# Index loads on other queues, routing and attention products in four groups of partitions, and a new order at the start of a four-layer graph network kernel

## The chip, the cores and the metric

The kernel runs on one core of a Trainium2 chip. The metric is the device time of one execution in microseconds (us), the median over runs; lower is better. A core has a matrix engine (TensorE, PE in the profile, with its weight loads listed as PEld), a vector engine (VectorE, DVE), a scalar engine (ScalarE, ACT), a general engine (GpSimd, POOL), a sequencer for transfers (SyncE, SP) and 16 DMA engines that these queues share. The whole program is one launch of about 40,000 instructions.

## The reference

512 nodes with 768 features pass four layers, and every layer adds a graph network, a token mixer and a feed-forward part to `x`. All four graph networks use the same list of 8704 edges (`src`, `dst`, two edge types, and 256 features for each edge). Cut to what the change touches:

```python
edge_index = jnp.stack([src, dst])
xn = _layernorm(x, axis=-1)
# layer 0, graph network: edges are projected, and summed at their destination
edge_proj = edge_features @ We.T + be
msgs = nodes[src] + nodes[dst] + edge_proj
agg = jax.ops.segment_sum(msgs, dst, num_segments=n)
...
# layers 0 and 2, feed-forward: each token goes to one of 8 experts
logits = xt @ Ws + bs
routes = jnp.argmax(jax.nn.softmax(logits, axis=-1), axis=-1)
...
# layers 1 and 3, graph network: attention over edges from two projections per node and head
qi = oi @ q ; kj = oj @ k
alpha = jax.nn.leaky_relu(qi + kj, NEG_SLOPE)
...
# layer 3, feed-forward: 16 experts, each takes its 64 best tokens
scores = jax.nn.sigmoid(x @ gate_weight.T)
topk_score, topk_ids = jax.lax.top_k(scores.T, capacity)
```

## The kernel before

The program is traced in Python and its instructions are ordered by a list scheduler. The scheduler keeps an order for each engine. It takes what it thinks is ready first, and among ready instructions what the program writes first. At run time every engine executes its own list in that order, and semaphores hold an instruction back until its inputs are there. A tile whose memory belonged to a closed pool waits for the last user of that memory. `tc.issue_after(i)` puts what its block traces on the engine of `i` behind `i` in that engine's list, without a wait.

**Start (`Net.__init__`, L179 to L221).** POOL issues the load of `x` (1536 KB) and of `cols` (all small columns of weights and biases, 210 KB), and then makes constants. Four constants are made on DVE: `sel`, `identb`, `lower` and part of `number`.

**Counting (`counts`, L371 to L516).** The four index arrays come in by POOL's queue (L391) and are cast to float (`ind`, L392). `worth` (L399 to L401) encodes the edge types. The edges lie in 68 columns of 128. For each column `j` DVE makes a one-hot `ohd` of its destinations (L465) and three weighted one-hots `so` of its sources (L468, three buffers). PE multiplies them into six accumulators (L471). This is done in four quarters, for `h` (half of the sources) and `g` (half of the columns): 34 columns with six bf16 products of 512 columns each. The accumulators are opened by a product with `onesb` (L462). At the end of a quarter ACT and DVE take the accumulators apart into digits (L236, L238, L478 to L449). Then follows a quarter of the 34 calls of `features(q)` (L411 to L425): a load of two columns of edge features `ea` (two buffers, by SP), a split of them into three bf16 parts on ACT and DVE alternately (L416, L417, L418, L419), and twelve products with `ohd` (L424). In the program `net.norm` of the first layer (L359 to L363) comes after `counts`, but its inputs are ready early.

**Narrow products.** In six places `xn` transposed (`xnT`, six chunks of 128 x 512, float32) is multiplied by a weight with only 6 to 24 columns, by `self.acc` (L320): the routers of `moe` in layers 0 and 2 (8 columns, `wg`, from `cols`), the attention projections of `rgat` in layer 1 twice (24 and 6 columns, `V`), of `gnn3` in layer 3 (24 columns), and the router of `ffn3` (16 columns, `gw`, from `cols`). The result has one row for each weight column and 512 columns. It is copied out (`loT`, `qkT`) and turned to one row per node by four transposes `self.tr` (L325).

**Order around them.** In `moe` and `ffn3` everything that follows needs the router's result, so PE has nothing else to do. In `rgat` and `gnn3` a generator (`side`, or `beside`) runs between other products on PE. In `ffn3` the weights of the experts (384 loads of 1152 KB) stream by SP into ten buffers `w`; SP issues a load as soon as a buffer is free. `ffn3` calls `rank` for the first two experts, then `choose`, `gather` and the first `up` (L1794), which frees the first buffers. The tile `first` (L1655) is a small sigmoid whose only purpose is to have the table of that function in ACT.

Of the kernel before, what the change touches and what calls it, by code (L numbers as in the profile page):

```python
# [10 lines left out]
F32 = mybir.dt.float32  # L11
# [63 lines left out]

def _layout(i):
# [32 lines left out]
    for f, n, g in (("f0", "L0_ffn", "Ws"), ("f2", "L2_ffn", "Wg")):  # L109
        col(f + "_wg", _thin(i[f"{n}_{g}"]))  # L110
        a[f + "_w1"] = np.stack([_blocks(w)[0, 0] for w in i[n + "_W1"]])
        a[f + "_w2"] = _rows(i[n + "_W2"])
        a[f + "_b2"] = np.ascontiguousarray(i[n + "_b2"])
        col(f + "_b1", _col(i[n + "_b1"]))
# [31 lines left out]
    col("f3_gw", _thin(i["L3_ffn_gate_weight"].T))  # L146
# [18 lines left out]
class Net:  # L165
    def __init__(self, ctx, tc, dram, at, out):
        self.tc, self.nc, self.d, self.at, self.out = tc, tc.nc, dram, at, out
        nc = self.nc
        self.cw = ExitStack()
        self.wp = self.cw.enter_context(tc.tile_pool(name="wp", bufs=6, side="right"))  # L170
        self.keep = ctx.enter_context(tc.tile_pool(name="keep", bufs=1))
        self.small = ctx.enter_context(tc.tile_pool(name="small", bufs=4))
        self.rowp = self.cw.enter_context(tc.tile_pool(name="rowp", bufs=2, side="right"))
        self.pp = ctx.enter_context(tc.tile_pool(name="pp", bufs=8, space=PSUM))
        self.dp = ctx.enter_context(tc.tile_pool(name="dp", bufs=1, space=DRAM))
        self.turn = 0
        keep = self.keep
        self.x = keep.tile([P, NT, D], F32, name="x")
        nc.gpsimd.dma_start(self.x, dram["x"].rearrange("(t p) d -> p t d", p=P))  # L179
        self.cols = keep.tile([P, dram["cols"].shape[1]], F32, name="cols")  # L180
        nc.gpsimd.dma_start(self.cols, dram["cols"])
        self.ident = keep.tile([P, P], F32, name="ident")
        make_identity(nc, self.ident)


        self.sel = keep.tile([96, 32], BF16, name="sel")
        for i in range(3):
            nc.vector.tensor_copy(self.sel[32 * i : 32 * i + 32, :], self.ident[:32, :32])
        self.bias3 = self.rowp.tile([96, 2, D], BF16, name="bias3", bufs=1)
        nc.gpsimd.memset(self.bias3, 0.0)  # L190
        self.which = 0
        self.ones = keep.tile([P, P], F32, name="ones")
        nc.gpsimd.memset(self.ones, 1.0)
        self.eps = keep.tile([P, 1], F32, name="eps")
        nc.gpsimd.memset(self.eps, LN_EPS)
        self.shift = keep.tile([P, 1], F32, name="shift")
        nc.gpsimd.memset(self.shift, -0.472)

        self.io16 = keep.tile([P, 16], F32, name="io16")
        nc.gpsimd.iota(self.io16, pattern=[[1, 16]], base=0, channel_multiplier=0, allow_small_or_imprecise_dtypes=True)  # L200
        self.io8 = self.io16[:, :8]
        self.me = keep.tile([P, 1], F32, name="me")
        nc.gpsimd.iota(self.me, pattern=[[0, 1]], base=0, channel_multiplier=1, allow_small_or_imprecise_dtypes=True)
        self.identb = keep.tile([P, P], BF16, name="identb")
        nc.vector.tensor_copy(self.identb, self.ident)
        self.big0 = keep.tile([P, 1], F32, name="big0")
        nc.gpsimd.memset(self.big0, -BIG)
        self.onesb = keep.tile([P, P], BF16, name="onesb")
        nc.gpsimd.memset(self.onesb, 1.0)
        self.wq1 = keep.tile([P, KC, 32], F32, name="wq1")  # L210
        self.gate = None
        self.lower = keep.tile([P, P], BF16, name="lower")
        with tc.tile_pool(name="init", bufs=1) as ip:
            io = ip.tile([P, P], F32, name="io")
            nc.gpsimd.iota(io, pattern=[[1, P]], base=0, channel_multiplier=0, allow_small_or_imprecise_dtypes=True)
            nc.vector.tensor_scalar(self.lower, io, self.me, None, OP.is_gt)

        self.number = keep.tile([P, NT, 2], BF16, name="number")
        nc.vector.tensor_copy(self.number[:, :, 0], self.me.to_broadcast([P, NT]))
        for t in range(NT):  # L220
            nc.gpsimd.memset(self.number[:, t, 1:2], float(t * P))  # L221

# [98 lines left out]

    def tr(self, out, in_):

        k = in_.shape[0]
        self.nc.tensor.transpose(out, in_, self.ident[:k, :k])  # L325
# [26 lines left out]
    def norm1(self, x, out, t):  # L352
# [8 lines left out]
        nc.scalar.activation(r, mv[:, 1:2], AF.Sqrt, bias=self.eps)  # L361
# [9 lines left out]
    def counts(self, c0, g0):  # L371
# [10 lines left out]
        with ExitStack() as c:  # L382
# [7 lines left out]
            for n, a in enumerate(("src", "dst", "edge_type_3", "edge_type_4")):  # L390
                nc.gpsimd.dma_start(raw[:, n, :], d[a].rearrange("(p j) -> p j", p=P))  # L391
# [10 lines left out]
            io = one.tile([P, N], I16, name="io")  # L402
            nc.gpsimd.iota(io, pattern=[[1, N]], base=0, channel_multiplier=0)
# [6 lines left out]
            def features(q):  # L410
# [7 lines left out]
                nc.scalar.copy(part[:, 1], ea)  # L418
# [38 lines left out]
            for h in range(2):  # L457
                digit = {}
                for g in range(2):
# [3 lines left out]
                    for j in range(g * HJ, (g + 1) * HJ):  # L463
# [3 lines left out]
                        for n in range(3):  # L467
                            nc.vector.tensor_scalar(so[:, n, :], io[:, h * 256 : (h + 1) * 256], ind[:, 0, j : j + 1],  # L468
                                                    worth[:, n, j : j + 1], OP.is_equal, OP.mult)
# [3 lines left out]
                    for (t, n), p in acc.items():  # L473
# [12 lines left out]
                        if g == 1:  # L486
                            finish(h, t, n, lo, hi, *digit[t, n])

                    for q in range((2 * h + g) * EJ // 8, (2 * h + g + 1) * EJ // 8):
                        features(q)  # L490
# [199 lines left out]
    def moe(self, f, act, xn, bs=None):  # L690
# [5 lines left out]
        with ExitStack() as c:  # L696
            one = c.enter_context(tc.tile_pool(name=f + "_one", bufs=1))
            two = c.enter_context(tc.tile_pool(name=f + "_two", bufs=2))
            xnT = one.tile([P, KC, N], F32, name="xnT")
# [8 lines left out]
            wg = self.col(f + "_wg", 0, KC * E).rearrange("p (k e) -> p k e", k=KC)  # L708
            p = self.ps()
            self.acc(p[:E], [(wg[:, k, :], xs[k]) for k in range(KC)])  # L710
            loT = one.tile([E, N], F32, name="loT")
            if bs is None:
                nc.vector.tensor_copy(loT, p[:E])
            else:
                nc.vector.tensor_scalar(loT, p[:E], self.col(bs, 0, 1, E), None, OP.add)
            p = self.ps()
            for t in range(NT):
                self.tr(p[:, t * E : (t + 1) * E], loT[:, t * P : (t + 1) * P])
            lo = one.tile([P, NT, E], F32, name="lo")
            nc.vector.tensor_copy(lo, p[:, : NT * E].rearrange("p (t e) -> p t e", t=NT))  # L720
# [423 lines left out]
    def fold(self, wq, l, H):  # L1144
# [19 lines left out]
        def turn(V, vt):  # L1164
            for a in range(2):
# [3 lines left out]
                nc.scalar.copy(V[:, 3 * a : 3 * a + 3],  # L1169
# [4 lines left out]
    def rgat(self, xT, l, H, V, C, done, between=None):  # L1174
# [4 lines left out]
        with ExitStack() as c:  # L1179
# [6 lines left out]
            qkT = one.tile([J, N], F32, name="qkT")  # L1186
# [8 lines left out]
            p = self.ps()  # L1195
            self.acc(p[:J], [(V[:, k].rearrange("p r h -> p (r h)"), xT[:, k, :]) for k in range(KC)])
            nc.scalar.copy(qkT, p[:J])
# [4 lines left out]
            def side():  # L1202
                p = self.ps()
                for t in range(NT):
                    self.tr(p[:, t * J : (t + 1) * J], qkT[:, t * P : (t + 1) * P])
                nc.scalar.copy(qk.rearrange("p t r h -> p (t r h)"), p[:, : NT * J])
                self.parts(qk3, qkT, qkT, mid, self.copies, nc.vector.tensor_sub)
# [60 lines left out]
    def gnn1(self, V1, xnT):  # L1268
        nc, tc, d = self.nc, self.tc, self.d
        with ExitStack() as c:  # L1270
# [34 lines left out]
            V2 = one.tile([P, KC, 3, 2], F32, name="V2")  # L1305
# [230 lines left out]
    def fold3(self, one):  # L1536
# [7 lines left out]
        V = one.tile([P, KC, 2 * H], F32, name="V")  # L1544
# [10 lines left out]
    def gnn3(self, c, xnT, V):  # L1555
# [19 lines left out]
        qkT = one.tile([2 * H, N], F32, name="qkT")  # L1575
# [5 lines left out]
        p = self.ps()  # L1581
        self.acc(p[: 2 * H], [(V[:, k, :], xnT[:, k, :]) for k in range(KC)])
        nc.scalar.copy(qkT, p[: 2 * H])
        for t in range(NT):
# [7 lines left out]
            if t == 0:  # L1592
                q = self.ps()
                for u in range(NT):
                    self.tr(q[:, u * 2 * H : (u + 1) * 2 * H], qkT[:, u * P : (u + 1) * P])
                nc.scalar.copy(qk.rearrange("p t r h -> p (t r h)"), q[:, : NT * 2 * H])
                self.parts(qk3, qkT, qkT, mid, self.copies, nc.vector.tensor_sub)
# [42 lines left out]
    def ffn3(self, xn, xnT, there):  # L1640
# [5 lines left out]
        with ExitStack() as c:  # L1646
# [8 lines left out]
            nc.scalar.activation(first, self.eps, AF.Sigmoid)  # L1655
# [10 lines left out]
            gw = self.col("f3_gw", 0, KC * NX).rearrange("p (k e) -> p k e", k=KC)  # L1666
            p = self.ps()
            self.acc(p[:NX], [(gw[:, k, :], xnT[:, k, :]) for k in range(KC)])
            loT = one.tile([NX, N], F32, name="loT")
            nc.vector.tensor_copy(loT, p[:NX])  # L1670
            p = self.ps()
            for t in range(NT):
                self.tr(p[:, t * NX : (t + 1) * NX], loT[:, t * P : (t + 1) * P])
            sc = one.tile([P, NT, NX], F32, name="sc")
            nc.scalar.activation(sc, p[:, : NT * NX].rearrange("p (t e) -> p t e", t=NT), AF.Sigmoid)
# [191 lines left out]
def tile_net(ctx, tc, dram, at, out, only=ALL):  # L1867
# [10 lines left out]
    with ExitStack() as ck, ExitStack() as c0:  # L1878
# [4 lines left out]
        with tc.tile_pool(name="L0", bufs=1) as pool:  # L1883
            xnT = pool.tile([P, KC, N], F32, name="xnT")
            with tc.tile_pool(name="L0n", bufs=1) as p2:
                xn = p2.tile([P, NT, D], F32, name="xn")
                net.norm(net.x, xn)
# [8 lines left out]
    with tc.tile_pool(name="L1", bufs=1) as pool, ExitStack() as keep:  # L1896
# [6 lines left out]
        V1 = pool.tile([P, KC, 3, 8], F32, name="V1")  # L1903
# [46 lines left out]
```

## Time and profile before

| | |
|---|---|
| median of 3 runs | 4281.39 us (4278.18 to 4281.85) |
| the profiled execution, its own time | 4283.03 us |
| its span, first to last instruction | 4281.2 us |
| mean granted TensorE clock | 0.988 |
| PE busy | 4117.0 us (96%) |
| DVE busy | 1299.7 us (30%) |
| ACT, POOL busy | 659.5 us (15%), 268.9 us (6%) |
| moved by DMA | 710.30 MB, 166 GB/s in the mean |

The span is what the trace covers; 1.8 us of the execution's own time lie around it. Busy time on PE counts pipelined matrix products until their modelled end, so 96% does not mean that PE runs at its peak. A share over the whole span says little here, because the stages have different limits: the first 25 us hardly use PE, and the last 1100 us move weights at 420 GB/s. So the prediction reads the stages one by one.

### The profile page before, as it was taken

What the parts mean: (1) busy time and instruction counts of PE and PEld (TensorE: products, weight loads), DVE (VectorE), ACT (ScalarE), POOL (GpSimd) and SP (SyncE); (2) the same over time, 40 slices, a digit from 0 to 9 for tenths busy, and PEclk for the clock granted to TensorE, in tenths of its full rate; (3) what the DMA queues carried; (4) which work ended last, traced back from release to release, by engine and by line L of the source; (5) the groups of instructions that cost most, each with busy time, mean ns of one, the idle gap of its engine ahead of it and who ended that gap; (6) DMA issues with size and microseconds to landing.
All of it is one profiled execution on the core that took longest, in us unless ns stands there. A gap on an engine that the chain in (4) does not pass through costs nothing. (4 is left out here: it accounts for less than half of the span.)

```text
span 4281.2 us, 40171 instructions
## 1 busy us (share of the span) xinstructions
PE 4117.0 (96%) x16392; PEld 2100.7 (49%) x16392; DVE 1299.7 (30%) x3120; ACT 659.5 (15%) x1241; POOL 268.9 (6%) x316
## 2 busy tenths in 40 slices
PE   7989999999989999999999999989999999999998
PEld 3434555554445566755644444445654444444443
DVE  7772111112432125513220101035841122122211
ACT  2121200001312223411200000022610000000000
POOL 1120000001022010000000000021100000000000
PEclk9999999999999999999999999989999999999999
DMA  3111011111047112211201111063079999999998
GB/s 111 52 61 57 23 45 66 67 56 53 18 169 293 38 60 72 107 45 55 106 34 67 45 55 56 0 261 136 1 288 420 419 420 420 420 417 420 419 421 363
DMA packets 98955, 710.30 MB, mean 166 GB/s; under 512 B 12032, under 2 KB 12096, under 8 KB 29392
## 3 DMA queue, kind: packets, MB, share of 16 engines
q1 hardware_dynamic: 77776, 601.13, 35.3%
q0 software_dynamic: 16512, 93.97, 5.8%
q10 hardware_dynamic: 4480, 12.58, 0.8%
q8 instruction: 132, 2.16, 0.2%
q14 instruction: 55, 0.45, 0.0%
HBM read 685.09 MB, written 22.54 MB: 165 GB/s over the span
## 5 line engine op out<-in xcount | busy, mean ns | idle before, releaser
L1794 PE MATMUL ps<-w,xg 128*64 128x384 f32 x3072 | 566.0, 489 | 5.0 <-DMA w<-in_f_Wg_dram 3.0
L1794 PEld LDWEIGHTS ps<-w,xg 128*64 128x64 f32 x3072 | 234.1, 137 | 297.2 <-issue 271.0
L1427 PE MATMUL ps<-aT,w 128*128 128x512 f32 x864 | 372.3, 592 | 0.0
L1810 PE MATMUL ps<-w,hT 128*64 128x384 f32 x1536 | 321.0, 490 | 6.3 <-ACT hT L238 2.5
L320 PE MATMUL ps<-xnT,w 128*128 128x512 f32 (+1 forms) x732 | 320.3, 594 | 0.3 <-ACT xnT L238 0.2
L1427 PEld LDWEIGHTS ps<-aT,w 128*128 128x128 f32 x864 | 164.2, 190 | 203.6 <-issue 202.3
L320 PE MATMUL ps<-w,xnT 128*128 128x384 f32 x672 | 221.6, 486 | 0.2 <-DVE xnT L236 0.2
L320 PEld LDWEIGHTS ps<-xnT,w 128*128 128x128 f32 (+1 forms) x732 | 133.7, 184 | 174.7 <-issue 171.3
L1810 PEld LDWEIGHTS ps<-w,hT 128*64 128x64 f32 x1536 | 132.1, 136 | 169.1 <-issue 143.9
L368 DVE TENSOR_TENSOR x<-x,ps 128x384 f32<-128x384 f32 x224 | 123.4, 553 | 295.0 <-PE ps L320 223.6
L320 PE MATMUL ps<-C,parts 128*128 128x512 bf16 x864 | 189.8, 381 | 4.0 <-DVE inv L1449 4.0
L320 PE MATMUL ps<-w,hT 128*128 128x384 f32 x552 | 184.7, 490 | 3.9 <-ACTq L895 3.9
L471 PE MATMUL ps<-ohd,so 128*128 128x512 bf16 x816 | 181.9, 383 | 2.8 <-DVE so L468 2.8
L320 PEld LDWEIGHTS ps<-w,xnT 128*128 128x128 f32 x672 | 127.0, 190 | 88.6 <-issue 4.7
L1437 DVE TENSOR_TENSOR aT<-inv,ps 128x512 f32<-128x512 f32 x72 | 49.5, 688 | 367.2 <-PE ps L320 367.2
L1797 ACT ACTIVATE h<-ps 128x384 f32<-128x384 f32 x64 | 31.4, 491 | 794.8 <-PE ps L1794 794.8
L1798 DVE TENSOR_TENSOR h<-h,ps 128x384 f32<-128x384 f32 x64 | 35.5, 554 | 377.6 <-PE ps L1794 377.6
L320 PEld LDWEIGHTS ps<-w,hT 128*128 128x128 f32 x552 | 103.1, 190 | 81.4 <-ACT xbT L238 7.6
L320 PE MATMUL ps<-w,aT 128*128 128x384 f32 (+1 forms) x416 | 139.6, 486 | 0.5 <-DVE aT L236 0.4
L320 PEld LDWEIGHTS <-parts 128*128 128x128 bf16 x864 | 84.9, 98 | 110.0 <-issue 11.0
L320 PE MATMUL ps<-xnT,sw 128*128 128x512 f32 x288 | 138.3, 611 | 0.0
L468 DVE TENSOR_SCALAR so<-io,ind,worth 128x256 bf16<-128x256 int16 x408 | 121.7, 355 | 35.5 <-PE ps L471 35.4
(499 smaller groups left out, 4804.4 us busy)
## 6 DMA issues: line engine op xcount, KB each, us to landing
w<-in_f_Wg_dram SPq DMA_DIRECT2D x128, 1152.0 KB, 14.5
w<-in_f_Wu_dram SPq DMA_DIRECT2D x128, 1152.0 KB, 15.2
w<-in_f_Wd_dram SPq DMA_DIRECT2D x128, 1152.0 KB, 16.0
w<-in_g_w_dram SPq DMA_DIRECT2D x54, 1152.0 KB, 5.1
w<-in_m_wqkv_dram SPq DMA_DIRECT2D x24, 1152.0 KB, 6.6
w<-in_g_t_dram SPq DMA_DIRECT2D x12, 1152.0 KB, 5.8
w<-in_m_wp_dram SPq DMA_DIRECT2D x8, 1152.0 KB, 5.3
ea<-in_edge_attr_dram SPq DMA_DIRECT2D x34, 256.0 KB, 2.7
```

Source lines behind the costliest of these rows:

```text
L320: self.nc.tensor.matmul(out, a, b, start=n == 0, stop=n == len(pairs) - 1)
L368: self.nc.vector.tensor_add(xs, xs, p)
L468: nc.vector.tensor_scalar(so[:, n, :], io[:, h * 256 : (h + 1) * 256], ind[:, 0, j : j + 1], worth[:, n, j : j + 1], OP.is_equal, OP.mult)
L471: nc.tensor.matmul(p, so[:, n, t * P : (t + 1) * P], ohd[:, j, :], start=False, stop=j == (g + 1) * HJ - 1)
L1427: nc.tensor.matmul(outs[nb * 3 + f], w[:, k, f * P : (f + 1) * P], xT[:, k, :], start=first and k == 0, stop=last and k == KC - 1)
L1437: nc.vector.tensor_mul(aT[:, f, :], inv[:, r, :], p)
L1794: nc.tensor.matmul(p[a * 64 : a * 64 + 64, :HW], xg[:, k, a * CAP : (a + 1) * CAP], ws[b][a][:, k, :], start=k == 0, stop=k == KC - 1)
L1797: nc.scalar.activation(h, pg[:, :HW], AF.Silu)
L1798: nc.vector.tensor_mul(h, h, pu[:, :HW])
L1810: nc.tensor.matmul(po[nb][a * 64 : a * 64 + 64, :HW], hT[:, f * P + a * 64 : f * P + a * 64 + 64], wd[a][:, f, nb * HW : (nb + 1) * HW], s ...
```

## The change

- **Indices.** The four index loads leave POOL's queue; `src` and `edge_type_3` go by SP, `dst` and `edge_type_4` by ACT. The int16 iota `io` and `onesb` are made first on POOL, ahead of the issue of `x` and `cols`.
- **Order of DVE at the start.** The four constants made on DVE move to a function `constants`, which is called with `net.norm` behind `begun`: the last `so` of the third quarter on DVE, and the last `part` of the second quarter on ACT. The DVE work of the first quarter's `features` stands behind the last `so` of the third column (`j` = 2).
- **Narrow products.** Weights are padded to 32 columns. The six chunks go to four groups of 32 output partitions (`narrow`): chunks 0 to 3 open a group each, chunks 4 and 5 add to groups 0 and 1. The four groups are added and turned to rows per node by four products with `fours`, four stacked 32 x 32 identities (`narrow_tm`). In `rgat` and `gnn3` one more product with `fours` makes the sum in rows per weight column.
- **Router weights.** `wg` and `gw` leave `cols` and get loads of their own (96 KB each): `wg` by ACT at the start of `moe`, `gw` by POOL in `ffn3`.
- **Sigmoid.** `first` stands behind `self.root`, the last square root of the norm before it on ACT.

```diff
+        self.onesb = keep.tile([P, P], BF16, name="onesb")
+        nc.gpsimd.memset(self.onesb, 1.0)
+        self.io = keep.tile([P, N], I16, name="io")
+        nc.gpsimd.iota(self.io, pattern=[[1, N]], base=0, channel_multiplier=0)
         nc.gpsimd.dma_start(self.x, dram["x"].rearrange("(t p) d -> p t d", p=P))
...
+        self.fours = keep.tile([P, 32], F32, name="fours")
+        for i in range(4):
+            nc.gpsimd.tensor_copy(self.fours[32 * i : 32 * i + 32, :], self.ident[32 * i : 32 * i + 32, 32 * i : 32 * i + 32])
...
+    def constants(self):
+        nc = self.nc
+        for i in range(3):
+            nc.vector.tensor_copy(self.sel[32 * i : 32 * i + 32, :], self.ident[:32, :32])
+        nc.vector.tensor_copy(self.identb, self.ident)
+        nc.vector.tensor_scalar(self.lower, self.io[:, :P], self.me, None, OP.is_gt)
+        nc.vector.tensor_copy(self.number[:, :, 0], self.me.to_broadcast([P, NT]))
...
+    def narrow(self, w, xs):
+        p = self.ps()
+        for k in range(KC):
+            g = 32 * (k % 4)
+            self.nc.tensor.matmul(p[g : g + 32], w[:, k, :], xs[k], start=k < 4, stop=k + 4 >= KC)
+        return p
+
+    def narrow_tm(self, four, n):
+        p = self.ps()
+        for t in range(NT):
+            self.acc(p[:, t * n : (t + 1) * n], [(four[:, t * P : (t + 1) * P], self.fours[:, :n])])
+        return p[:, : NT * n].rearrange("p (t n) -> p t n", t=NT)
...
-        nc.scalar.activation(r, mv[:, 1:2], AF.Sqrt, bias=self.eps)
+        self.root = nc.scalar.activation(r, mv[:, 1:2], AF.Sqrt, bias=self.eps).ins
...
             for n, a in enumerate(("src", "dst", "edge_type_3", "edge_type_4")):
-                nc.gpsimd.dma_start(raw[:, n, :], d[a].rearrange("(p j) -> p j", p=P))
+                (nc.sync, nc.scalar)[n % 2].dma_start(raw[:, n, :], d[a].rearrange("(p j) -> p j", p=P))
...
                         for n in range(3):
-                            nc.vector.tensor_scalar(so[:, n, :], ...
+                            if j == 3 and n == 0 and h == 0:
+                                made["third"] = made["so"].ins
+                            made["so"] = nc.vector.tensor_scalar(so[:, n, :], ...
...
+                    if h == 1 and g == 0:
+                        self.begun = made["so"].ins, made["part"].ins
                     for q in range((2 * h + g) * EJ // 8, (2 * h + g + 1) * EJ // 8):
-                        features(q)
+                        if h == g == 0:
+                            with tc.issue_after(made["third"]):
+                                features(q)
+                        else:
+                            features(q)
...
             # moe
+            wg = one.tile([P, KC, 32], F32, name="wg")
+            nc.scalar.dma_start(wg.rearrange("p k e -> p (k e)"), d[f + "_wg"])
...
-            self.acc(p[:E], [(wg[:, k, :], xs[k]) for k in range(KC)])
-            loT = one.tile([E, N], F32, name="loT")
+            p = self.narrow(wg, xs)
+            loT = one.tile([P, N], F32, name="loT")
...
-            for t in range(NT):
-                self.tr(p[:, t * E : (t + 1) * E], loT[:, t * P : (t + 1) * P])
-            nc.vector.tensor_copy(lo, p[:, : NT * E].rearrange("p (t e) -> p t e", t=NT))
+            nc.vector.tensor_copy(lo, self.narrow_tm(loT, E))
...
             # rgat, in side(); gnn3 alike
-                for t in range(NT):
-                    self.tr(p[:, t * J : (t + 1) * J], qkT[:, t * P : (t + 1) * P])
-                nc.scalar.copy(qk.rearrange("p t r h -> p (t r h)"), p[:, : NT * J])
-                self.parts(qk3, qkT, qkT, mid, self.copies, nc.vector.tensor_sub)
+                self.acc(p[:J], [(self.fours[:, :J], qkT)])
+                nc.scalar.copy(qk.rearrange("p t r h -> p t (r h)"), self.narrow_tm(qkT, J))
+                self.parts(qk3, p[:J], qkT[:J], mid, self.copies, nc.vector.tensor_sub)
...
             # ffn3
-            nc.scalar.activation(first, self.eps, AF.Sigmoid)
+            with self.tc.issue_after(self.root):
+                nc.scalar.activation(first, self.eps, AF.Sigmoid)
+            gw = one.tile([P, KC, 32], F32, name="gw")
+            nc.gpsimd.dma_start(gw.rearrange("p k e -> p (k e)"), d["f3_gw"])
...
+            p = self.narrow(gw, self.chunks(xnT))
+            loT = one.tile([P, N], F32, name="loT")
+            nc.vector.tensor_copy(loT, p)
             sc = one.tile([P, NT, NX], F32, name="sc")
-            nc.scalar.activation(sc, p[:, : NT * NX].rearrange("p (t e) -> p t e", t=NT), AF.Sigmoid)
+            nc.scalar.activation(sc, self.narrow_tm(loT, NX), AF.Sigmoid)
...
-                net.norm(net.x, xn)
+                with tc.issue_after(net.begun[0]), tc.issue_after(net.begun[1]):
+                    net.constants()
+                    net.norm(net.x, xn)
```

## The prediction

> **What bounds the kernel now.** I read the page's 40 slices first. PE is at 9 almost everywhere, so a gain has to come from PE time or from stretches where PE stands still. Then I asked for PE's waits and the timeline of the start, then for the timeline around each of the six narrow products, and last for the tables by stage. PE's waits between 25 and 345 us (columns: total, times, longest) begin with this:
>
> ```profile
> PE ps L424 <- DVE ohd L465: 17.1, 1, 17.1
> PE ps L424 <- DVE part L419: 5.9, 6, 2.9
> PE ps L424 <- ACT part L418: 4.5, 3, 3.5
> PE ps L471 <- DVE so L468: 2.8, 4, 1.3
> ```
>
> One wait of 17.1 us ends at the first one-hot. The timeline (start, us, engine, line) tells why it is late:
>
> ```profile
> 0.73 0.86 SPq L414 DMA_DIRECT2D ea<-in_edge_attr_dram  x2
> ...
> 3.62 1.24 ACT L416 CAST part<-ea 128x512 bf16<-128x512 f32 x2 [1.62 <-DMA ea<-in_edge_attr_dram]
> ...
> 7.09 1.06 POOL L391 DMA_DIRECT2D so<-in_edge_type_dram  x2
> ...
> 16.43 1.48 DVE L359 BATCH_NORM_STATS2 st<-x 128x6 f32<-128x384 f32 x3 [9.39 <-DMA x<-in_x_dram]
> ...
> 24.34 0.27 DVE L392 CAST ind<-so 128x272 f32<-128x272 int32 x1
> ...
> 27.70 12.65 PE L471 MATMUL ps<-ohd,so 128*128 128x512 bf16 x55
> ```
>
> DVE stands until 16.43 for `x`, since the norm is ahead of the indices in its list, and works off the norm and four constants until 24.3. The indices were issued last on POOL's queue, behind `x`. Then comes the cast. From 25.6 PE is the bound of the columns; only the ends of the second and fourth quarter are DVE's (stretch, then busy us of PE, PEld, DVE, ACT, POOL, clock, DMA share):
>
> ```profile
> 25.00:60.00 35.00, 34.39 (x152) 15.23 (x152) 34.20 (x136) 0.00 (x0) 0.00 (x0) 1.00 0.07 30
> ...
> 300.00:310.00 10.00, 8.01 (x24) 2.74 (x24) 10.00 (x18) 4.10 (x8) 3.37 (x4) 0.73 0.33 106
> ```
>
> The router of layer 0, and two other places where PE runs in column groups or on small outputs:
>
> ```profile
> 1226.62 5.32 PE L320 MATMUL ps<-xnT,cols 128*8 128x512 f32 x12 [0.24 <-DVE xnT L236]
> ...
> 1232.77 0.41 PE L325 MATMUL ps<-ident,loT 8*128 8x8 f32 x4 [0.83 <-DVE loT L715]
> ```
>
> ```profile
> 394.76 1.06 PE L555 MATMUL ps<-sq,half 96*32 96x512 f32 x6
> 395.75 1.10 PE L320 MATMUL ps<-xnT,w 128*96 128x512 f32 x2
> ...
> 1765.04 7.94 PE L1157 MATMUL ps<-w,wq 128*32 128x384 f32 x72
> ...
> 3206.86 0.95 PE L320 MATMUL ps<-number,oh 128*128 128x2 f32 x8
> ```
>
> A float32 product is two instructions. One of 512 columns passes in 0.43 us (5.32 / 12), eight columns wide or not. L1157 writes three groups of 32: 72 instructions in 7.94 us are 24 threes of 0.33, the price of one instruction of 384 columns alone. So groups overlap in full. In the last expert layer:
>
> ```profile
> 3146.32 1.28 ACT L1675 ACT_TABLE_LOAD   x1 [5.72 <-issue]
> ...
> 3170.00:3172.00 2.00, 2.00 (x16) 0.93 (x14) 0.00 (x0) 0.00 (x0) 0.00 (x0) 1.00 0.00 0
> ```
>
> The first line lies between the router's turned product and its sigmoid. The second is from a table of short stretches: DMA stands still from 3167.5 to 3173.0, because ten weights are loaded and the first `up` has freed none. After that DMA moves 420 GB/s to the end.
>
> **The change, part by part.** *Start.* The first `ea` landed 2.45 us after its issue ended (1.16 to 3.6). The second index load on SP ends its issue at 1.6, so it is there at 4.0 or before, being 34 KB and not 256. With ACT's table load (1.28) ahead of its two loads it would be 5.3; without the transfer time of 256 KB it would be 3.4. I take 4.0. `onesb` and `io` are made by 1.5, as the first of POOL's list; the issue of `x` and `cols` moves back by 0.8 (0.20 and 0.58), and nobody early needs them now. The six openings L462 (2.7) lie before 4.0. The cast then starts at 4.0 and not at 24.34, and what follows keeps its distance: 20.3 us gained (19 to 20.9).
>
> What is given back: (a) the DVE work of the first two `features`, 2 x 1.39 = 2.8 us, which before lay in the idle start, comes after the third column. Its cover is that DVE makes all 68 `ohd` in the first quarter, where 34 are needed: 34 x 0.27 = 9.2 us ahead. I count 0.5; without cover it is 2.8. (b) Norm and constants are 3.9 + 0.8 + 0.3 + 3.7 = 8.8 us of DVE (L359, L360, L362; L188, L205, L216, L219), now behind the last `so` of the third quarter. In the columns of the fourth quarter DVE works 0.86 of 1.295 us each, so 0.43 x 29 = 12.5 us are free. The list scheduler puts late program text into such gaps. I count 1.0; if it all falls into the DVE-bound end it is 8.8. Their square roots on ACT bring a table load of 1.28, where ACT is idle. The index issues on SP delay `ea` by 0.9, which nobody waits for. Net 18.8.
>
> *Routers of layers 0 and 2.* The chunks of `xnT` come in pairs from DVE and ACT, the last at 1227.77. Groups 0 and 1 then need one product each, together 0.86, plus 0.16 to the end: 1228.8 in place of 1231.94, 3.1 less. The copy `loT` costs the same on 128 rows (0.74 for 512 columns). The turn: the nearest row is L320 `number,oh`, eight instructions with 128 x 128 weights, 0.81 us to the next product, against 0.41 for the four transposes: 0.4 more. Gain 2.7 each, and all of it is on the path, since PE, DVE and the gathers of weights wait for `lo`. The load of `wg` stands in ACT's list at the start of `moe`. Its memory is free with the last product of the layer before (1222.5), so it lands near 1225.4, 1.2 before its use. Queued behind it on ACT would be the square root at 1224.25, for which DVE and the transposes wait; if ACT also stood at it for the earlier three, their 0.68 us scalings would pile up: 1 to 2 us, once.
>
> *`rgat` twice and `gnn3`.* PE is full there (20.00 of 20.00 us in each stretch from 1600 to 1740). 12 x 0.43 become 4 x 0.43: 3.5 less. The product for rows per weight column adds 0.86 and the turn 0.4: 2.2 gained each. In `gnn3` the chunks arrive until 2939.4, so 3.2 less, 1.9 net. `qk3` is cast 0.6 later on ACT, and its first reader on PE is 5 us behind. The sets to zero of `V` on POOL are 0.3 each, early.
>
> *`ffn3`.* Like the routers, plus the sigmoid: its table load moves behind the last square root (3137.30), where ACT is free until 3139: 1.28 gained. The weight `gw` goes by POOL at 3135.75, when that memory comes free (the iota does so now), just as eight weight loads start on SP.
>
> **A rule against a row.** The nearest row for `gw` is `x`: 1536 KB, issue over at 2.22, landed at 16.43 beside SP's weights, 14.2 us. [...] By the row, a quarter as many row pieces (128 of 512) between equally many big ones take 14.2 / 4 = 3.6[...]. I take 3140.6, so the product ends at 3142.5 and not 3145.0. With 2.5 - 0.4 + 1.28 that is 3.4 gained[...]. The DMA pause of 5.5 us is longer than either, so the stream to the end starts earlier by all of it.
>
> **A second rule.** [...] The row: L555, six instructions in three groups, should take 0.86, and the next full-width product starts 0.99 after their start. So a switch is at most 0.13, and 12 switches at most 1.6 us. [...] I take the row, and nothing, since 5.32 for 12 holds such an end too.
>
> **Sum.** 18.8 + 2.7 + 2.7 + 2.2 + 2.2 + 1.9 + 3.4 = 33.9 us. Against the profiled execution's own 4283.0 us that is 4249.1; the median of the runs is 1.6 lower, so I predict 4247.5.
>
> **Rivals.** *The DVE-bound end* (14%): norm and constants are not put into the gaps and lie before the digits of the fourth quarter: 7.8 more, 4255. For it: DVE is 10.00 of 10.00 busy there. Against: 12.5 us of gaps just before. *A feature stall at the start* (11%): `features` 2 and 3 load behind five loads `w` (until 18 us), while PE's fixed order wants them earlier; up to 8 us of waiting, 4255. Against: before, all but three early feature products stood behind the 204 column products. *Groups do not overlap* (5%): products in several groups of one bank follow one another. Then what the six products were to lose (3.1 + 3.1 + 3.5 + 3.5 + 3.2 + 2.5 = 18.9 us) stays, and their added work too: 4266. L1157 speaks against it. *The feature chain becomes the bound, slower* (4%): the place is the four stretches of `features`. With two `ea` buffers one call passes load, ACT, DVE, ACT, DVE. At 300 to 314 us a call takes about 4.1 us, in the PE-paced stretch from 82.7 to 95.1 it takes 2.7. If the new DVE work, wedged between these steps, made all 34 calls as slow, it would cost 34 x 1.4 = 48 us, and the result would be 4296. It decides from 3.7 us per call, where the 34 us are eaten up. Against: DVE's list changes only in the first and the last quarter. *That the change does not do what it says*: the index loads could stand behind `ea` and the weights in SP's list, which costs 1 to 3 us and is in my range.
>
> **Numbers.** The forecast has 66%, with 4239 to 4254 of its own (the start 19 to 20.9, the give-back 0 to 4, each narrow product to 0.6 either way). The two rivals at 4255 are taken in with the same width, up to 4261; the third and the slower one are left out. A measurement of this kernel can tell about 0.2% (8.6 us) from no change. All cases but the last are faster by more than that, and a third case that comes with losses at the start lies within 0.2%.
>
> **What would show it.** Right: the cast L392 near 4 us, the first L471 near 5.7, PE without a long wait until the first digits, the product with `EFT` (before at 328.35) near 309; six groups of 12 instructions of 128*32 in about 2 us each; no ACT_TABLE_LOAD between `loT` and `sc`; a DMA pause of 2 us in `ffn3`. Wrong: BATCH_NORM_STATS2 among the last digits, PE waiting for `part` before 50 us, 5 us for a 128*32 group, or PE waiting for `gw`.

## The result, and the profile after

The changed kernel takes 4256.82 us (median of 5 runs, 4255.87 to 4260.7) beside 4281.85 (5 runs, 4278.18 to 4285.66) of the kernel before: a ratio of 0.9943, 95% interval 0.9929 to 0.9958, or 25.0 us. The forecast was 33.9 us (4247.5), so 9 us are missing. That is outside the 4239 to 4254 of the forecast itself, and inside the whole range, which went to 4261 for two rivals. The profiled execution spans 4255.0 us.

First PE's waits of the changed kernel from 4 to 340 us (columns: total, times, longest):

```profile
PE ps L451 <- DVE part L446: 10.6, 10, 3.3
PE ps L451 <- ACT part L445: 4.2, 3, 3.1
PE ps L500 <- DVE so L497: 3.9, 5, 1.3
PE ps L451 <- DVE ohd L492: 2.5, 1, 2.5
```

The wait of 17.1 us for the first one-hot is 2.5 now. The waits for `part`, mostly at the ends of the second and fourth quarter, are 14.8 us in all (10.4 before). They cost little: between 72 and 328 us the changed kernel loses 0.5 us against the kernel before (table below). PE's granted clock was at half for 17.1 us of that part before and is so for 6.8 now. The wait for `so` is small as a wait, but part of it lies in the first quarter, where there was none. The first column product of the kernel before:

```profile
26.42 1.06 PE L471 MATMUL ps<-ohd,so 128*128 128x512 bf16 x2
```

The start of the changed kernel (start, us, engine, line):

```profile
3.09 1.41 POOL L198 MEMSET bias<- 96x1536 bf16 x1
...
3.94 0.72 DVE L420 CAST ind<-so 128x272 f32<-128x272 int32 x1 [2.56 <-DMA so<-in_edge_type_dram]
...
7.06 9.32 PE L500 MATMUL ps<-ohd,so 128*128 128x512 bf16 x36
...
13.27 1.50 DVE L497 TENSOR_SCALAR so<-io,ind,worth 128x256 bf16<-128x256 int16 x3
...
13.86 0.82 POOL L290 CAST bias<-row 1x768 bf16<-1x768 f32 x1 [0.17 <-DMA row<-in_m_bv_dram]
...
14.77 2.01 POOL L291 TENSOR_TENSOR row<-row,bias 1x768 f32<-1x768 f32 x1
15.21 4.14 DVE L497 TENSOR_SCALAR so<-io,ind,worth 128x256 bf16<-128x256 int16 x3
16.74 0.81 POOL L290 CAST bias<-row 1x768 bf16<-1x768 f32 x1
...
17.64 1.63 POOL L291 TENSOR_TENSOR row<-row,bias 1x768 f32<-1x768 f32 x1
...
19.27 0.87 DVE L492 TENSOR_SCALAR ohd<-io,ind 128x512 bf16<-128x512 int16 x3
```

The cast starts at 3.94, as forecast, 20.4 us earlier, and the first column product at 7.06: 19.4 us are there. (The line at 27.70 in the prediction is the third column product; two stand ahead of it.) But the columns of the first quarter, 45.9 us before (26.42 to 72.36), now take 50.9 (7.06 to 57.92). Three `so`, 0.86 us otherwise, take 1.50 and then 4.14 us, and the 4.14 end at 19.27, where POOL's second subtraction ends. POOL splits two bias rows there for a product that comes 300 us later.

By stretches of 2.5 us (stretch; length; busy us of PE, PEld, DVE, ACT, POOL with instructions; granted clock; DMA share; GB/s):

```profile
15.00:17.50 2.50, 1.77 (x8) 0.51 (x6) 2.50 (x4) 0.00 (x0) 2.50 (x2) 1.00 1.02 424
17.50:20.00 2.50, 0.98 (x4) 0.41 (x5) 2.50 (x5) 0.00 (x0) 1.68 (x2) 1.00 1.00 409
20.00:22.50 2.50, 2.50 (x8) 0.75 (x6) 2.50 (x11) 0.00 (x0) 0.00 (x0) 0.52 1.02 424
22.50:25.00 2.50, 2.50 (x11) 1.03 (x10) 2.50 (x11) 0.00 (x0) 0.00 (x0) 0.80 0.98 409
```

PE gets 12 products through where 23 belong, and after the pause its clock falls to 0.52: the next products stand 0.43 us apart and not 0.216.

Layer 0's router, and the last expert layer:

```profile
1211.11 2.25 PE L340 MATMUL ps<-xnT,wg 128*32 128x512 f32 x12 [0.24 <-DVE xnT L249]
...
1214.24 1.06 PE L333 MATMUL ps<-fours,loT 128*128 128x8 f32 x8 [0.88 <-DVE loT L751]
```

```profile
3112.15 0.54 POOL L1688 DMA_DIRECT2D gw<-in_f_gw_dram  x1 [17.03 <-PE ps L333]
3112.16 0.81 SPq L257 DMA_DIRECT2D w<-in_f_Wg_dram  x2
...
3113.79 1.28 ACT L1686 ACT_TABLE_LOAD   x1
...
3118.06 1.91 PE L340 MATMUL ps<-xnT,gw 128*32 128x512 f32 x12 [2.44 <-DMA gw<-in_f_gw_dram]
...
3121.91 0.22 ACT L1703 ACTIVATE sc<-ps 128x64 f32<-128x64 f32 x1 [5.13 <-issue]
```

Twelve instructions pass in 2.25 us (5.32 before). In `ffn3` the table load is out of the way, but PE waits 2.44 us for `gw`, which landed 5.8 us after its issue.

Where the time goes is seen best by the distance between two traces: how much earlier the same group of products starts than in the kernel before. Single places vary between traces by up to 2.3 us: the changed kernel and the one with gw by ACT have the same order of instructions up to 3090 us, and stand at 17.9 and 15.6 at the first router. What a single part gains is therefore read from the distance just before and just after it.

| place (us in the kernel before) | changed | start only | POOL later | gw by ACT | both |
|---|---|---|---|---|---|
| columns of first quarter done (72.36) | 14.5 | 14.2 | 18.4 | 13.8 | 17.7 |
| product with EFT (328.35) | 13.9 | 12.7 | 17.1 | 13.3 | 16.3 |
| mix0 (424.38) | 15.4 | 14.1 | 18.5 | 13.6 | 16.2 |
| first router done (1234.80) | 17.9 | 14.4 | 21.1 | 15.6 | 18.6 |
| both rgat done (1784.17) | 21.7 | 15.0 | 25.9 | 20.3 | 24.0 |
| second router done (2809.88) | 24.5 | 15.1 | 27.5 | 23.7 | 25.2 |
| gnn3's product done (2946.68) | 25.1 | 15.2 | 29.2 | 24.4 | 26.9 |
| in gnn3 (3009.49) | 23.8 | 15.1 | 29.1 | 24.1 | 26.8 |
| ranks of ffn3 begin (3147.89) | 25.7 | 15.1 | 29.6 | 27.9 | 30.6 |
| end (4247.96) | 25.9 | 16.5 | 30.2 | 30.1 | 31.7 |

The other four columns are experiments.

### The profile page after: what moved, and what is told of

Its sections match the earlier page's. It is cut to its first block, busy times and chain, and to the rows that moved or that the text cites. A ratio compares the mean times of both kernels' runs of the same rounds, so it can differ in the third digit from the quotient of the medians.

```text
span 4255.0 us, 40231 instructions
## 1 busy us (share of the span) xinstructions
PE 4105.1 (96%) x16422; PEld 2102.8 (49%) x16422; DVE 1301.0 (31%) x3120; ACT 658.4 (15%) x1240; POOL 269.5 (6%) x318
## 4 chain that ended last, share of the span: by engine, by line
PE 63%; DVE 3%; DMA 2%; issue 0%; ACT 0%; POOL 0%; DVEq 0%; ACTq 0%; POOLq 0%; SPq 0%
PE ps L333 30%; PE ps L1822 12%; PE ps L1459 11%; PE ps L1838 6%; PE ps L353 2%; PE ps L1290 1%; DMA w<-in_f_Wd_dram 1%; PE ps L1271 1%; DVE pt L1052 0%; DVE e L1051 0%; PE ps L1190 0%; DMA w<-in_g_t_dram 0%; PE ps L340 0%; DVE inv L1482 0%; DVE qk L1544 0%
## 6 DMA issues: line engine op xcount, KB each, us to landing
w<-in_f_Wg_dram SPq DMA_DIRECT2D x128, 1152.0 KB, 14.2
w<-in_f_Wu_dram SPq DMA_DIRECT2D x128, 1152.0 KB, 14.1
```

## The experiments

Each is an edit of the changed kernel. The kernel before took 4281.85 us beside the changed kernel, and 4280.6, 4280.8 and 4281.4 in the three groups of experiments, so medians can be compared across them to about 1 us.

**The start alone.** The narrow products, their weights and turns, and the sigmoid are put back:

```
-            p = self.narrow(wg, xs)
+            p = self.ps()
+            self.acc(p[:E], [(wg[:, k, :], xs[k]) for k in range(KC)])
...
```

> The changed kernel with the six narrow products, their turns, their weights and the sigmoid's table load as they were before; only the start is changed. My theory: the 25 us are two sums that don't touch each other, 13.9 us of the start (328.35 to 314.43 at the product with EFT) and about 11 us of the six narrow products. Then this kernel takes 4281.9 - 13.9 = 4268, the product with EFT begins within 0.5 us of 314.4, and from there on the distance to the kernel before stays within 2 us of 13.9. Rival: part of what the later traces show at 422 us and after is no work of the narrow products but a later consequence of the start (weights that were loaded earlier); then the time is 4262 to 4265 and the distance grows behind 330 us. Second rival: the start's gain is lost again in stretches that other things pace; then 4272 or more.

4264.95 us, ratio 0.9963 (0.9949 to 0.9976): 15.7 us. EFT's product is 12.7 us early, not 13.9; from mix0 to the end the distance stays between 14.1 and 16.5. So the two parts hardly touch each other: 15 to 16 us of the 25 are the start, 9 to 10 the narrow products. The time lies in the first rival's range, and 1.4 us are indeed gained at 400 to 424 us without any narrow product. But that is the clock, not a part of the change. In the kernel before the granted clock was at half from 421.5 to 424.9 us. In the traces that gain here (changed, start only, POOL later) it stays at full at this place; in gw by ACT and both repairs, which gain 0.3 and nothing, it falls to half here too (from 408.4 and from 405.1, 3.4 us each).

**POOL's splitting later.** Both splittings wait for an `so` of the third quarter, where DVE has a third of its time free:

```
+                        if h == 1 and j in (6, 18):
+                            self.late.append(made["so"].ins)
...
+            r = self.nc.gpsimd.tensor_copy(o, i)
+            if self.late:
+                self.tc.add_manual_dep(r.ins, self.late.pop(0).name, ...)
```

> The changed kernel, with the first two splittings of bias rows (m_bv, m_bp; CAST and TENSOR_TENSOR on POOL, 13.86 to 19.27 us) made to wait for two one-hots of the third quarter, near 175 and 190 us, where DVE has a third of its time free. Theory: POOL's work holds DVE up. Then the rows of three `so` take 0.86 us throughout (1.50 and 4.14 before), PE waits for no `so` in the first 50 us (2.25 us in all in the changed kernel), the granted clock is 1.00 from 20 to 25 us (0.52 and 0.80), the first quarter's columns end 3.5 to 5 us earlier, and the kernel takes 4252 to 4253.5. In the third quarter DVE's rows beside POOL get longer, but PE waits less than 0.5 us there. Rival: the x, cols and weight loads, which fill the DMA engines (share 1.0) from 7 to 25 us, or the clock are the cause; they stay as they are, so the slow rows and the pause stay within 0.5 us of the changed kernel's and the time is 4256.8.

4252.44 us, ratio 0.9933 (0.9919 to 0.9946). The same stretches of this kernel:

```profile
15.00:17.50 2.50, 2.50 (x14) 1.12 (x12) 2.50 (x11) 0.00 (x0) 0.00 (x0) 1.00 1.03 428
17.50:20.00 2.50, 2.45 (x12) 1.13 (x12) 2.50 (x10) 0.00 (x0) 0.00 (x0) 1.00 1.01 412
20.00:22.50 2.50, 2.50 (x13) 1.16 (x12) 2.50 (x11) 0.00 (x0) 0.00 (x0) 1.00 1.01 420
```

The DMA share is 1.0 as before, and yet nothing is slow: neither the loads nor the clock were the cause, POOL was. The first quarter ends 4 us earlier. In its new place POOL holds DVE up as well, but there the stock of `so` covers it: four `so` tiles take 4.80 us and not 3.4, and PE goes on without a break:

```profile
177.68 7.50 PE L510 MATMUL ps<-ohd,so 128*128 128x512 bf16 x33
...
178.59 0.81 POOL L288 CAST bias<-row 1x768 bf16<-1x768 f32 x1 [18.80 <-DVE so L505]
178.96 4.80 DVE L505 TENSOR_SCALAR so<-io,ind,worth 128x256 bf16<-128x256 int16 x12 [0.44 <-PE ps L510]
179.48 1.63 POOL L299 TENSOR_TENSOR row<-row,bias 1x768 f32<-1x768 f32 x1
```

How POOL's work holds DVE up, the traces do not show. They show that the 4.14 us of three `so` in the changed kernel end at 19.27, with POOL's second subtraction. The trace of before had it already, where it slowed the constants, in front of the cast of the indices:

```profile
19.70 1.63 POOL L278 TENSOR_TENSOR row<-row,bias 1x768 f32<-1x768 f32 x1
...
20.58 1.74 DVE L188 CAST sel<-ident 32x32 bf16<-32x32 f32 x3
...
22.18 1.63 POOL L278 TENSOR_TENSOR row<-row,bias 1x768 f32<-1x768 f32 x1
22.33 1.57 DVE L205 CAST identb<-ident 128x128 bf16<-128x128 f32 x1
```

In the changed kernel the same casts, now at 201 us and away from these rows of POOL, take 0.53 and 0.23 us (1.74 and 1.57 above).

There is a third place, which no experiment moves on purpose: the cast of the indices itself, 0.72 us and not 0.27. POOL sets `bias` to zero beside it, from 3.09 to 4.50. In all eleven traces with the new start the cast begins somewhere between 3.43 and 4.00 and ends 0.16 us after POOL's row. In the kernel with gw at the start POOL's row ends 0.54 us later, and so does the cast (5.04 and 5.20).

**gw by ACT.** One word is changed, the queue:

```
-            nc.gpsimd.dma_start(gw.rearrange("p k e -> p (k e)"), d["f3_gw"])
+            nc.scalar.dma_start(gw.rearrange("p k e -> p (k e)"), d["f3_gw"])
```

> The changed kernel with the load of gw (in ffn3) issued by ACT in place of POOL, at the same place of the program and with the same memory, which comes free near 3112. Theory A: the queue of POOL makes it late. ACT's load of wg in the first moe layer landed 2.1 us after its issue; gw then lands before 3115.5, PE waits for it under 0.3 us and ffn3 begins 2.4 us earlier: 4254.4. Theory B: the DMA engines are shared with eight weight loads that SP issues from 3112.16 on; a load of 384 KB... of 96 KB in 128 rows takes its turn between them whatever queue it is in, lands 4 us or more after its issue, and PE waits 1.2 us or more: 4256.

4252.54 us, ratio 0.9934 (0.992 to 0.9948). It lands 2.7 us after its issue, and PE does not wait for it:

```profile
3111.60 0.34 ACTq L1688 DMA_DIRECT2D gw<-in_f_gw_dram  x1
...
3111.82 0.80 SPq L257 DMA_DIRECT2D w<-in_f_Wg_dram  x2
...
3115.57 2.20 PE L340 MATMUL ps<-xnT,gw 128*32 128x512 f32 x12 [0.29 <-issue]
```

From gnn3 to the ranks the distance grows by 3.8 us, beside 1.9 in the changed kernel. That looked like theory A. But the issue also slipped 0.22 us in front of the weights. The next experiment tells the two apart.

**gw by ACT, behind the weights.** The same load, tied behind the last square root:

```
+            with self.tc.issue_after(self.root):
+                nc.scalar.dma_start(gw.rearrange("p k e -> p (k e)"), d["f3_gw"])
```

> The changed kernel with gw issued by ACT behind the last square root (near 3113.8), so that it is issued 1.6 us after the first of SP's eight weight loads and not just ahead of them. It tells apart why the load landed 2.7 us after its issue on ACT's queue and 5.8 us on POOL's. Theory A, the queue: it lands 2.7 us after its issue here too, near 3116.5; PE waits for it about 1 us and not 2.4, and the kernel takes 4255.5. Theory B, the place in the order: in the run with ACT's queue it was issued 0.22 us ahead of the weights, here it comes behind them; it lands 5 us or more after its issue, near 3119, and PE waits 3 us or more: 4257.5.

4260.97 us, ratio 0.9956 (0.994 to 0.9971). Landing took 8.1 us:

```profile
3113.58 0.34 ACTq L1687 DMA_DIRECT2D gw<-in_f_gw_dram  x1
...
3121.86 3.63 PE L340 MATMUL ps<-xnT,gw 128*32 128x512 f32 x12 [6.30 <-DMA gw<-in_f_gw_dram]
```

So theory A fell: on one and the same queue the place in the order makes 5.4 us. This small load waits behind the big ones: it lands after 2.7 us just ahead of the weights (2.0 with both repairs), 5.8 level with them, 8.1 at 1.5 us behind. The packets in the traces say the same: the first one of `gw` moves 1.0 us after the issue ahead of the weights, 3.7 us after it on POOL's queue level with them, 3.6 us after it on ACT's queue behind them. No run issued it from POOL ahead of the weights, so a smaller share of that queue is not excluded. Theory B's time was still 3.5 us too low: PE waits 6.30 us, and the product takes 3.63 us after that and not 2.2.

**gw at the start**, into memory that stays:

```
+        self.gw = keep.tile([P, KC, 32], F32, name="gwk")
+        nc.gpsimd.dma_start(self.gw.rearrange("p k e -> p (k e)"), dram["f3_gw"])
```

> The changed kernel with gw loaded at the start of the kernel by POOL, third in its list behind x and cols, into memory that it keeps, so that no load lies in front of the product of ffn3. Theory: PE's 2.44 us of waiting for gw is all that keeps the narrow product back. Then the product starts when the first pair of xnT is there (2.4 us earlier than in the changed kernel), the pass of 12 instructions takes about 2.3 us as in the moe layers and ends at or soon after the last pair of xnT, so the gain is 2 to 2.4 us: 4254.6. What POOL does at the start comes 0.6 us later, at no cost. Rival: the stretch behind is paced by the weights that SP loads from 3112 on (DMA share 1.0 until 3144); then the router is earlier but the end is not, and the time is 4256 to 4257.

4253.83 us, ratio 0.9938 (0.9924 to 0.9951). From gnn3 to the ranks the distance grows by 3.7 us (25.09 to 28.76), and 27.9 to 29.0 us are left towards the end: the stream of weights does not swallow it.

**The sigmoid untied.** The line with `issue_after(self.root)` is left out.

> The changed kernel with the first sigmoid of ffn3 no longer tied behind the last square root; ACT then does it long before, as in the kernel before, and loads the table again between loT and sc. Theory: the load of 1.28 us stands in front of sc and PE waits for sc, so ffn3 begins its ranks 1.28 us later than in the changed kernel: 4258, and one more table load early that costs nothing. Rival: the wait for gw hides the load, so that it costs nothing here: 4256.8.

4258.7 us, ratio 0.9948 (0.9933 to 0.9963), 1.9 us slower than the changed kernel; the runs of the two overlap. A load of 1.28 us stands again between the turned product and `sc`. From gnn3 to the ranks 1.2 us are lost where the changed kernel gained 1.9: 3.1 us between them, of which 1.28 are the load, and 1.7 the product, which took 3.59 us behind a wait for `gw` of 2.56. So the load is not hidden in this trace.

**The norm untied.** `issue_after(net.begun[0])` and `[1]` are left out; DVE then does constants and norm at the end of the first quarter.

> The changed kernel with the norm and the constants no longer tied behind the last `so` of the third quarter; by its list DVE then does them near the end of the first quarter's columns, and the first square roots stand on ACT before the digits of the first quarter. The prediction counted 1.0 us for the tied place and 8.8 if all of it fell into a stretch that DVE bounds. Theory A: 8.8 us of DVE work in front of the digits come back as a wait of PE at the openings of the second quarter, since those need the sums copied away: 4 to 9 us slower, 4261 to 4266. Theory B: behind the first quarter PE has 23 us of feature products, in which DVE has little to do, so the work is hidden there as it is in the third quarter: within 1.5 us of the changed kernel, 4256 to 4258.

4259.6 us, ratio 0.9952 (0.9937 to 0.9967), 2.8 us slower; the runs overlap here too. Neither theory hits. At 139 us the distance is 11.6 and not 13.6, so the place costs 2.0 us; 1.5 come back as a wait for ACT's `part`. The rest of the DVE work is hidden. It is less than the 8.8 us counted: two of its casts took 3.3 us before beside POOL and take 0.75 here, which leaves about 6.2. In the tied place the changed kernel loses nothing: 13.6 at 287 us, 13.9 at EFT.

**The first features untied.** `issue_after(made["third"])` is left out.

> The changed kernel with the first quarter's features no longer tied behind the third column's one-hots; by its list DVE then does the four subtractions of the first two features (2.8 us) ahead of the first column's successors. Theory A: PE has nothing else to do in that time, and the columns of the first quarter give DVE no slack (1.30 to 1.40 us of DVE for 1.30 of PE each), so the end of the first quarter comes 2 to 3 us later: 4259 to 4260. Theory B: DVE is ahead by then with one-hots that only the second quarter needs, so it catches up: within 0.7 us of the changed kernel. Theory C: the values of `ea` and ACT's casts are not there when DVE reaches them, since the indices now go first in both queues; DVE stands longer than the 2.8 us, 4 us or more are lost: 4261.

4261.58 us, ratio 0.9957 (0.9942 to 0.9972). Theory C: DVE stands behind `ea`, which lands late now, and PE behind DVE.

```profile
9.14 0.62 ACT L443 CAST part<-ea 128x512 bf16<-128x512 f32 x1 [3.61 <-DMA ea<-in_edge_attr_dram]
...
9.79 0.69 DVE L444 TENSOR_TENSOR ea<-ea,part 128x512 f32<-128x512 f32 x1 [2.84 <-ACT part L443]
...
12.18 0.59 PE L451 MATMUL ps<-ohd,part 128*128 128x512 bf16 x1 [8.03 <-DVE ohd L492]
```

The first quarter ends 5 us later (distance 9.4 beside 14.5). Without tying them a third of the start's gain would be gone.

**Both repairs**: POOL's splitting later, and gw by ACT ahead of the weights.

> The changed kernel with both repairs: the splittings of the two bias rows on POOL wait for one-hots of the third quarter, and gw is issued by ACT. Theory: the two losses (4.3 us at the end of the first quarter, 2 us in ffn3) have nothing to do with each other, so their gains add up: the start gains 18.4 us against the kernel before at the end of the first quarter (72.36 there), ffn3 3.8 us, and the time is 4249 to 4250.5, a ratio of about 0.9925 to the kernel before. Rival: one of them only shifts where PE waits, or the stream of weights to the end takes its own time; then the time is that of either one alone, 4252.5.

4249.3 us (4249.13 to 4251.8), ratio 0.9929 (0.9915 to 0.9942): 31.5 us faster than the kernel before. The intervals of the ratios overlap with the changed kernel's, but no run of the one lies among those of the other (4255.87 to 4260.7), and the distance at the end is 31.7 and not 25.9. The two add up.

**The additions on DVE.** In the kernel with both repairs POOL and DVE also meet at the ends of the quarters:

```profile
292.67 3.99 POOL L476 TENSOR_TENSOR AT<-AT,S 128x512 f32<-128x512 f32 x1 [3.77 <-DVE S L470]
...
298.50 0.69 DVE L482 TENSOR_TENSOR s<-AT,s 128x512 f32<-128x512 f32 x1 [1.28 <-POOL AT L477]
```

```
-                nc.gpsimd.tensor_add(A, S[:, 0, :], S[:, 1, :])
+                nc.vector.tensor_add(A, S[:, 0, :], S[:, 1, :])
...
```

> The kernel with both repairs, and the three additions for AT at the end of the second and of the fourth quarter done by DVE and not by POOL. DVE bounds these ends; in the profile of the kernel with both repairs its rows beside POOL's additions are 1.16, 1.37, 1.75 and 1.91 us long and not 0.69, one addition on POOL takes 3.99 us and not 1.3, and DVE then waits 1.28 us for it. Theory: on DVE each addition takes 0.6 us and nothing is held up: six more per end are 3.6 us, but 3.5 us of longer rows, 1.3 us of waiting, and the late `most` go, so that each end is 1 to 2 us shorter: 4246 to 4248. Rival: DVE's longer rows have been off the path that sets the end; then its 3.6 us more per end count, and the time is 4252 to 4256.

4261.84 us, ratio 0.9956 (0.9942 to 0.9969): 12.5 us slower than with both repairs, far off both numbers. The DVE rows that were 1.16 to 1.91 us long are 0.68 now, so the holding-up is gone. But the list scheduler then placed all digits ahead of the features' subtractions, and PE stood once at this end for a whole chain (and once for 5.9 us in the second quarter):

```profile
PE ps L459 <- ACT part L453: 17.0, 1, 17.0
```

What the additions on DVE would cost in an unchanged order stays open.

## Why the prediction was right, and where it was off

The range holds by luck in part: 4256.82 lies outside the forecast's own 4239 to 4254, and the part up to 4261 was there for two rivals that did not come. The signs of the parts are right, most sizes are too large.

**The start, 20.3 gross:** the cast is at 3.94 (4.0 forecast), 20.4 us earlier. But "what follows keeps its distance" fails at once: the first column product is 19.4 us earlier. The cast took 0.72 us and not 0.27, beside POOL's row, and DVE's list now holds all of `worth` ahead of the first `ohd`, which begins 2.3 us after the cast and not 0.9. (The 5.7 named for the first column product does not follow from that either: 26.42 less 20.3 is 6.1.)

**Net 18.8:** mis-sized; 13.9 at EFT. The step that failed is the same one, which moved everything and let "what follows keep its distance". The columns of the first quarter take 4.9 us more. What moved now meets POOL's splitting: 3.9 us of it, shown by moving POOL away; the remaining 1.0 is not taken apart. The prediction's own line for 25 to 60 us had the warning: DVE is busy for 34.20 of 35.00 us there, so what holds DVE up holds PE up. With both repairs 16.3 are left at EFT, with POOL alone moved 17.1. PE's own start differs between the traces: its first products stand 0.43 us apart, 8 of them in the changed kernel (to 9.96 us) and 8 in the kernel before as well (25.61 to 28.96), but 14 with both repairs (to 12.57), 1.3 us more. The clock column shows 1.00 there only because the record of the clock begins where this ends (9.86, 28.93 and 12.52 us). What ends this slow stretch, and why it is longer in one trace than in another, was not tested.

**(a), features, 0.5 of 2.8:** right. With POOL away PE waits once, 0.3 us, for a `so` in the first 56 us. That holds only for the tied place.

**(b), norm, 1.0:** nearer 0, and 2.0 where DVE would put it by itself. The 8.8 us of work behind it were too many: two casts in them were long only because of POOL.

**Routers, 2.7 each:** 2.3 and 2.4. The last pair of `xnT` sets the product's end, as forecast; the copy `loT` took 0.75 and 0.69 us on 128 rows, where it took 0.74 and 0.68 on 8; the turn took 1.06 us where four transposes took 0.41, so 0.65 more and not 0.4. **rgat, 2.2 each:** 1.9 in each of four traces. The next product starts 1.85 us after the first of the twelve instructions, and four times 0.43 are 1.72, so the changes to column groups and back take 0.13 us together at most (the prediction's bound was 0.13 for each). **gnn3, 1.9:** 0.8 to 1.2. The product gained 2.9 and not 3.2, and the product for rows with the turn cost 1.5 and not 1.3; in the changed kernel's own trace it is lost again behind the product, where the clock is at half for 6.8 us (from 2976.0; before for 3.4, from 3001.9), and in the others it stays.

**ffn3, 3.4:** mis-sized; 1.9. The step is the landing of `gw`. Counted from the end of its issue, as in the prediction, it landed after 5.3 us. The row of `x` gave 3.6, and the 4.3 that were taken (to 3140.6) were the author's estimate; both were too early. The row treats the load by its pieces, while its place in the order decides (2.7, 5.8 and 8.1 us from issue to landing). So PE waited 2.4 us and not 0.9 (from the first chunk, at 3139.7 before, to 3140.6). With `gw` in time the term is 3.7 to 3.8, more than the 3.4 of the forecast. The 1.28 us of the table load were right.

**Sum of the changed kernel:** 13.9 (start) + 1.4 (by 424 us, the clock) + 2.3 + 3.8 + 2.4 + 1.9, and nothing from gnn3, are 25.7; 25.9 is the distance at the end.

**Rivals:** none came. The end that DVE bounds did not take the norm, groups overlap (twelve instructions in 1.91 to 2.25 us in the changed kernel, 5.32 before), and the slower feature chain did not appear; what it would need, features in front, was seen only when they were untied. Of the lines named as wrong, one is there: PE waiting for `gw`.

## What to carry to other kernels

When a change moves a stretch of work in time, look at what the idle engines do at the new place: the stretch itself was costed well, its neighbours were not. POOL work that nobody needs soon belongs where DVE has slack, not beside the first DVE-paced columns (here 4252.44 us beside 4256.82). A small load that a product needs is issued ahead of a stream of big ones, or long before (here it landed 2.7 us after its issue just ahead of them, 5.8 level with them and 8.1 behind).

## What was not expected of the hardware

DVE stood for up to 3.3 us behind POOL's work on a single row of 768 elements (4.14 us in place of 0.86), and POOL beside DVE (3.99 in place of 1.3, while DVE worked without a gap; this one was not tested apart).

A pause of PE cost twice in the first quarter. After 2.25 us of waiting (0.55, 0.38 and 1.32) the granted clock was at half from 20.10 to 23.52 us, and the products there stood 0.43 us apart. With POOL's splitting moved away PE waits 0.3 us for `so` up to 56 us, and the clock is 1.00 in every stretch from 7 to 54 us. In `ffn3` the twelve instructions behind the wait for `gw` took 3.45, 2.81, 2.94, 3.59 and 3.63 us in five kernels that waited 2.33, 2.38, 2.42, 2.56 and 6.30 us, and 1.91 us in the changed kernel, which waited 2.44; its granted clock stays at full until 3122.82. So the length of the wait alone does not decide; what does is not shown.
